# ScalarE's queue in the first feed-forward product: the activations of a unit's lower half put behind the copy of its upper half

## The chip, the cores and the metric

The kernel runs on one core of one Trainium2 chip. The metric is the device time of a whole execution in microseconds (us), lower is better. Times of engines, waits and transfers come from one profiled execution of the kernel; TensorE is called PE in the profile (its weight loads PEld), VectorE DVE, ScalarE ACT, GpSimd POOL, and SyncE, which issues the DMAs, SP (its issuing side SPq).

## The reference

128 graphs of 128 nodes with 256 features go through two layers, all in fp32. Layer 0: two rounds of graph attention (a masked softmax over a 128x128 score matrix, times the features), a residual and a layer norm, a feed-forward block with ReLU, a residual and a layer norm. Layer 1: multi-head attention with eight heads and values by relation, a residual and a norm, a feed-forward block with GELU, a residual and a norm. What the change touches is the first product of each feed-forward block and its activation:

```python
ff = jnp.matmul(jax.nn.relu(jnp.matmul(h, w_ff1) + b_ff1), w_ff2) + b_ff2        # layer 0
ff = jax.nn.gelu(x @ W1 + b1, approximate=False) @ W2 + b2                        # layer 1
```

`h` and `x` are 128 x 128 x 256, the hidden width is 1024.

## The kernel before

Four graphs make a group (`G = 4`), so there are 32 groups, and each goes through five stages: the loads, the graph attention `gat` (L421), the feed-forward block of layer 0 (`ff0`), the attention of layer 1 (L453) and the feed-forward block of layer 1 (`ff1`). Each stage is a Python generator that yields its planned duration at many points; a heap (L654 to L676) always resumes the stage whose planned time is lowest, so the stages of neighbouring groups are interleaved with a fixed period: while one group is in `ff0`, an earlier one is in attention and `ff1`, a later one in `gat`. From planned time 280 on (`kept`, L57) the PE's instructions, and SP's throughout, are tied to this order of emission by manual dependencies (L671). The queues of ACT, DVE and POOL are not tied: the framework's scheduler sets them when the program is built. The adjacency holds only 0 and 1, so the arm that runs is the one planned by `BINARY`.

The first product of a feed-forward block is a 2x2 block product with seven instead of eight block multiplications (`moving_sums`, L299, and `weight_sums` prepare the sums). Its hidden width is done in two units (`unit(0)` and `unit(2)`, L357, called u0 and u1 here), each resumed four times in turn (L358). In one unit:

- products 1 and 5 go into two PSUM tiles, `chain` and `side`; ACT copies them out (L333, L334);
- products 6, 2 and 3 follow: 6 is added onto `chain` in PSUM, 3 onto `side`. ACT copies `chain` out (L340), DVE adds the rest to make both parts of the lower half `lo` (L341, L342);
- product 7 is added onto `chain`; ACT copies it out (L345) for the second part of the upper half `hi`, which POOL completes (L346); ACT applies the activation to `lo` (L348, two instructions of 128x512);
- product 4 is added onto `chain`: it may start only when the copy of L345 has read `chain`. ACT then applies the activation to the four parts of `hi` (L354), two from `chain`, two from POOL's result.

The second product (L372) reads `lo` and `hi` of u0 first, then of u1. The same function serves both layers: in `ff0` the activation is ReLU, in `ff1` GELU. [...]before GELU and again before the exponentials of the attention (L498) a table is loaded (`ACT_TABLE_LOAD`).

Other work that the text names:

- L485, the score matmuls of the attention, PE; per group one set of 32 for its first two graphs and two of 16 for the others. Then L489 (row maxima, DVE), L498 (exponentials, ACT, 16 or 8 instructions), L502 and L503 (DVE, POOL), and the transposition of the weights by L282 (DVE), L285 (four DMAs out to DRAM) and L287 (one DMA back, tile `eT`). L517 (DVE) masks `eT`, L534 (DVE) moves the values `v` out of PSUM, and L546 (PE) multiplies `v` by the two; L550 (ACT) copies its result for L577 (PE).
- The layer norm `normalised` (L244): L250 and L251 (DVE), four short POOL instructions of which L257 is the last, and L259 (ACT, four of 128x256).
- `gat`: L429 and L437 (PE) give `wh`, which ACT copies out (L430, L438); L397 (DVE) turns one column of `wh` into `zs`, L399 (SP) writes it to DRAM and L401 reads it back over all rows; L404 (ACT) needs it, then L411 to L413 (DVE), L416 (ACT), L417 (DVE), L418 (POOL). L382 (DVE) adds the second product of a feed-forward block to the residual.

Of the kernel before, what the change touches and what calls it, by code (L numbers as in the profile page):

```python
# [214 lines left out]
def stages_of(tc, a, out, c, pools, plan):  # L215

    nc = tc.nc
# [26 lines left out]
    def normalised(y, first=0, n=G):  # L244

        y = y[:, first:first + n]
        mv = sm.tile([P, n, 2], F32, name="mv")
        for b in range(n):
            st = sm.tile([P, 6], F32, name="st")
            nc.vector.bn_stats(st, y[:, b])  # L250
            nc.vector.bn_aggr(mv[:, b], st)  # L251
        rstd = sm.tile([P, n], F32, name="rstd")
        nc.gpsimd.tensor_scalar(rstd, mv[:, :, 1], EPS, None, op0=OP.add)
        nmr = sm.tile([P, n], F32, name="nmr")
        nc.gpsimd.tensor_scalar(nmr, mv[:, :, 0], -1.0, None, op0=OP.mult)
        nc.gpsimd.tensor_tensor(rstd, rstd, c.mhalf[:, :n], OP.pow)
        nc.gpsimd.tensor_mul(nmr, nmr, rstd)  # L257
        for b in range(n):
            nc.scalar.activation(y[:, b], y[:, b], AF.Identity, bias=nmr[:, b:b + 1], scale=rstd[:, b:b + 1])  # L259

    def affine(y, k, b, n, engine=nc.gpsimd):


        for op, v in zip((OP.mult, OP.add), c.ln[k]):
            engine.tensor_tensor(y[:, b:b + n], y[:, b:b + n], v[:, None, :].to_broadcast([P, n, D]), op)  # L265
# [26 lines left out]
    def features(y, direct):  # L292

        t = t_tile().rearrange("p (b c n) -> p b c n", b=G, c=DC)
        blocks = t.rearrange("p b c n -> p (b c) n")
        transposed(y.rearrange("p b (c f) -> p (b c) f", f=P), blocks, direct, blocks)
        return t

    def moving_sums(hT):  # L299

        b11, b21, b12, b22 = (hT[:, h:h + G // 2, c] for h in (0, G // 2) for c in range(DC))
        t1, t2, t4 = (wk.tile([P, G // 2, N], F32, name=f"t{i}") for i in (1, 2, 4))
        nc.gpsimd.tensor_sub(t1, b12, b11)  # L303
        nc.gpsimd.tensor_sub(t2, b22, t1)
        nc.gpsimd.tensor_sub(b12, b22, b12)
        nc.gpsimd.tensor_sub(t4, t2, b21)
        return None, b11, b21, b22, t4, t1, t2, b12

    def feed_forward(y, before, direct, win, bin_, wout, func, by=G):


        hT = features(y, direct)
        yield TIMES["lead ff0" if before == "01" else "lead ff1"]
        hs = moving_sums(hT)
        yield TIMES["sums"]
        fT = [None] * FC

        def unit(f0):

            lo, hi = (wk.tile([P, 2, 2, T // 2], F32, name="fT", bufs=FC // 2) for _ in range(2))  # L320
            for i in range(2):
                fT[f0 + i] = lo[:, i].rearrange("p h t -> p (h t)")
                fT[FC // 2 + f0 + i] = hi[:, i].rearrange("p h t -> p (h t)")

            def product(p, k, first=False):
                for i in range(2):
                    nc.tensor.matmul(p[:, i], win[k][:, ts(f0 + i, P)], hs[k], start=first and i == 0, stop=True,  # L327
                                     skip_group_check=True)

            chain, side = (ps.tile([P, 2, T // 2], F32, name="mm") for _ in range(2))  # L330
            product(chain, 1, True)
            product(side, 5, True)
            nc.scalar.copy(lo[:, :, 0], chain)  # L333
            nc.scalar.copy(hi[:, :, 0], side)  # L334
            yield
            p = ps.tile([P, 2, T // 2], F32, name="mm")
            product(chain, 6)
            product(p, 2, True)
            product(side, 3)
            nc.scalar.copy(lo[:, :, 1], chain)  # L340
            nc.vector.tensor_add(lo[:, :, 0], lo[:, :, 0], p)  # L341
            nc.vector.tensor_add(lo[:, :, 1], lo[:, :, 1], side)  # L342
            yield
            product(chain, 7)
            nc.scalar.copy(hi[:, :, 1], chain)  # L345
            nc.gpsimd.tensor_add(hi[:, :, 1], hi[:, :, 1], hi[:, :, 0])  # L346
            for i in range(2):
                nc.scalar.activation(lo[:, i], lo[:, i], func, bias=bin_[:, f0 + i:f0 + i + 1])  # L348
            yield
            product(chain, 4)  # L350
            for h, p in enumerate((chain, hi[:, :, 1])):
                for i in range(2):
                    f = FC // 2 + f0 + i
                    nc.scalar.activation(hi[:, i, h], p[:, i], func, bias=bin_[:, f:f + 1])  # L354
            yield

        units = [unit(0), unit(2)]  # L357
        for n, now in enumerate(((0,), (1,), (0,), (1,), (0,), (1,), (0,), (1,))):  # L358
            for u in now:
                next(units[u])  # L360
            if n in (2, 4):
                affine(y, before, n - 2, 2)
            yield TIMES["ff visits"][n]
        yield TIMES["ff2"]

        late = sorted(range(FC), key=lambda f: f % (FC // 2) // 2)
        ys = [ps.tile([P, 2, D], F32, name="mm") for _ in range(G // 2)]

        def second(b, part):

            for n, f in part:
                nc.tensor.matmul(ys[b // 2][:, b % 2], fT[f][:, ts(b, N)], wout[:, f],  # L372
                                 start=b % 2 == 0 and n == 0, stop=n == FC - 1, skip_group_check=True)

        order = list(enumerate(late))
        for b in range(G):
            second(b, order[:FC // 2])
        yield TIMES["ff first half"]
        for k in range(0, G, 2):
            for b in (k, k + 1):  # L380
                second(b, order[FC // 2:])
            nc.vector.tensor_add(y[:, k:k + 2], y[:, k:k + 2], ys[k // 2])  # L382
            yield TIMES["ff half"]
            if (k + 2) % by == 0:
                normalised(y, k + 2 - by, by)
        return y
# [202 lines left out]
    def ff0(y, direct):  # L589
        return feed_forward(y, "01", direct, c.wf1_sums, c.col["bf1"], c.wf2, AF.Relu)  # L590

    def ff1(y, direct, by):
        return feed_forward(y, "11", direct, c.w1_sums, c.col["b1"], c.w2, AF.Gelu, by)
# [5 lines left out]
def layers(ctx: ExitStack, tc: tile.TileContext, a: dict, out: bass.AP, c, plan: dict):  # L599
# [3 lines left out]
    TIMES, PERIOD = plan["times"], plan["period"]  # L603
    pools = Pools(ctx, tc, plan["bufs"])
    gat_block, ff0, attention, ff1, affine, load_group = stages_of(tc, a, out, c, pools, plan)
    x0, x1, x2, loads = dict(enumerate(c.y)), {}, {}, {}

# [72 lines left out]
def graph_layers(ctx: ExitStack, tc: tile.TileContext, a: dict, out: bass.AP):  # L680
# [17 lines left out]
    with ExitStack() as start:  # L698
        tmp = start.enter_context(tc.tile_pool(name="tmp", bufs=1))
        pools = Pools(start, tc, BINARY["bufs"])  # L700
        others = constants(tc, a, c, cst, tmp, pools.ps)
        gat_block = stages_of(tc, a, out, c, pools, BINARY)[0]
        gats = [gat_block(True, f"wh{g}", g, c.xt[g], c.at[g], c.y[g]) for g in range(LEAD)]
        while gats:
            gats = [s for s in gats if next(s, None) is not None]

        words = a["adjT"].rearrange("g p b n -> (g p b n)").rearrange("(k p w) -> k p w", p=P, k=4)
        top = tmp.tile([P, 4], F32, name="top")
        for k in range(4):
            t = tmp.tile([P, words.shape[2]], I32, name="scan", bufs=3)  # L710
            nc.sync.dma_start(t, words[k])
            nc.vector.tensor_reduce(top[:, k:k + 1], t.bitcast(U32), AX.X, OP.max)
        others()
        folded(nc, c, pools.ps, c.wf1, c.col["bf1"], "01")
        c.wf1_sums = weight_sums(nc, c, c.wf1, "wf1")

        ones = tmp.tile([P, 1], F32, name="ones")
        nc.vector.memset(ones, 1.0)
        other = tmp.tile([P, 1], F32, name="other")
        nc.vector.tensor_reduce(other, top, AX.X, OP.max)  # L720
        nc.vector.tensor_scalar(other, other, 1.0, None, op0=OP.is_gt)
        p = pools.ps.tile([1, 1], F32, name="mm")
        nc.tensor.matmul(p, other, ones, start=True, stop=True)
        nc.vector.tensor_copy(flag, p)
        found = nc.values_load(flag[0:1, 0:1], min_val=0, max_val=P,
                               skip_runtime_bounds_check_because="it counts partitions")
# [54 lines left out]
```

## Time and profile before

| what | value |
|---|---|
| median of 3 runs | 2922.73 us (2919.74 to 2925.28) |
| the profiled execution | 2924.12 us, of which the span of the trace is 2922.3 us |
| mean granted PE clock | 0.978 |
| PE, DVE, ACT, POOL busy | 94%, 52%, 57%, 55% of the span |
| DMA | 328.83 MB, 49.1% of 16 engines' span |

The 40 slices of the span show PE at 90% or more from the fifth slice to the 38th; before and after these lie a start of some 90 us (loads and the first two groups alone) and an end in which nothing is left to interleave with. Between them the same pattern repeats once per group, every 84.0 to 88.1 us. A line of the timeline gives start, duration, engine, line, operation, tile written and tiles read, and in brackets how long the engine had been idle and what released it. PE's busy time is high throughout, so its few waits are what to look at.

### The profile page before, as it was taken

Reading aid. Unit: us, or ns where it says so; the run is one execution under the profiler, and the core shown is the slowest. Engines: PE = TensorE matmul, PEld = TensorE weight load, DVE = VectorE, ACT = ScalarE, POOL = GpSimd, SP = SyncE. Lnnn points to the kernel's source line nnn. Section 1 sums busy time; section 2 is a strip of 40 time slices with the busy share of each in tenths; the row PEclk is TensorE's granted clock in tenths of the full one; section 3 lists DMA queues with packets and bytes.
Section 4 is the critical chain, followed back from the end, with each engine's and each line's share of the span. In section 5 each row is a group of like instructions: output and inputs, shape, how many; then the busy total and the mean of one; then the engine's idle time right before and its main releaser. Section 6 shows DMA issues by size and latency. Waiting matters only on the chain.

```text
span 2922.3 us, 47504 instructions
## 1 busy us (share of the span) xinstructions
PE 2756.2 (94%) x16578; PEld 2146.2 (73%) x16578; DVE 1519.8 (52%) x3193; ACT 1674.7 (57%) x5127; POOL 1598.6 (55%) x1866
## 2 busy tenths in 40 slices
PE   4996999999999999999999999999999999999988
PEld 3764777777877777777777777777777777777766
DVE  5444455555544545555555565455565555455442
ACT  3445556566666565655655665656665565665543
POOL 1424555566655556655645665655566565556553
PEclk7998999999999999999999999999999999999999
DMA  7145445565455556545445555445655544554310
GB/s 274 44 105 117 100 98 112 119 135 127 109 116 109 111 117 137 113 113 119 105 106 133 121 111 119 107 108 122 134 116 115 121 107 109 125 130 107 78 37 15
DMA packets 1156955, 328.83 MB, mean 113 GB/s; under 512 B 903008, under 2 KB 1126752, under 8 KB 1156064
## 3 DMA queue, kind: packets, MB, share of 16 engines
q1 hardware_dynamic: 1156704, 325.68, 49.1%
q8 instruction: 134, 2.20, 0.3%
q14 instruction: 117, 0.96, 0.1%
HBM read 195.97 MB, written 129.62 MB: 111 GB/s over the span
## 4 chain that ended last, share of the span: by engine, by line
PE 55%; ACT 13%; DVE 11%; DMA 10%; issue 4%; SPq 4%; POOL 2%; DVEq 0%; ACTq 0%; POOLq 0%
PE mm L372 22%; PE mm L327 11%; PE mm L533 5%; ACT e L498 4%; DMA eT<-zd 4%; SPq L285 3%; PE av L546 3%; PE mm L462 3%; PE mm L469 3%; ACT tok L259 3%; PE mm L577 2%; DVE st L250 2%; DMA zd<-e 2%; DMA zd<-T 2%; PE mm L429 2%
## 5 line engine op out<-in xcount | busy, mean ns | idle before, releaser
L265 POOL TENSOR_TENSOR tok<-tok,ln_rows 128x512 f32<-128x512 f32 (+1 forms) x596 | 669.4, 1132 | 33.5 <-DVE T L282 11.5
L498 ACT ACTIVATE e<-mm,nm 128x128 f32<-128x128 f32 x1024 | 360.5, 392 | 241.4 <-DVE nm L489 225.8
L372 PE MATMUL mm<-wf,fT 128*128 128x256 f32 x2048 | 464.1, 383 | 8.6 <-ACT fT L354 7.4
L372 PE MATMUL mm<-w,fT 128*128 128x256 f32 x2048 | 460.6, 381 | 0.0
L372 PEld LDWEIGHTS mm<-wf,fT 128*128 128x128 f32 x2048 | 386.8, 191 | 73.1 <-ACT fT L354 16.1
L372 PEld LDWEIGHTS mm<-w,fT 128*128 128x128 f32 x2048 | 386.6, 190 | 70.3 <-issue 20.5
L517 DVE TENSOR_TENSOR m<-eT,am 128x1024 f32<-128x1024 f32 x128 | 184.0, 1439 | 447.6 <-DMA eT<-zd 447.4
L503 POOL TENSOR_TENSOR e<-e,s 128x512 f32<-128x512 f32 x256 | 268.5, 1057 | 253.9 <-DVE s L502 253.9
L489 DVE TENSOR_REDUCE nm<-mm 128x2 f32<-128x256 f32 (+1 forms) x384 | 171.6, 502 | 250.9 <-PE mm L485 250.9
L348 ACT ACTIVATE fT<-fT,col 128x512 f32<-128x512 f32 x256 | 170.4, 715 | 206.8 <-DVE fT L342 203.0
L259 ACT ACTIVATE tok<-tok,nmr,rstd 128x256 f32<-128x256 f32 x480 | 248.9, 590 | 46.7 <-POOL nmr L257 46.5
L418 POOL TENSOR_TENSOR e<-e,s 128x512 f32<-128x512 f32 (+1 forms) x68 | 68.1, 1003 | 342.6 <-DVE s L417 319.5
L533 PE MATMUL mm<-wv,T 128*128 128x512 f32 x512 | 247.6, 606 | 0.0
L346 POOL TENSOR_TENSOR fT<-fT 128x512 f32<-128x512 f32 x128 | 162.5, 1271 | 151.4 <-ACT fT L345 151.4
L498 ACT ACTIVATION_READ_ACCUMULATOR e<-mm,nm 128x1 f32 x1024 | 237.0, 231 | 0.0
L303 POOL TENSOR_TENSOR t<-T 128x256 f32<-128x256 f32 x64 | 47.6, 743 | 327.9 <-DMA T<-zd 327.9
L327 PE MATMUL mm<-T,w 128*128 128x256 f32 x768 | 203.9, 388 | 5.8 <-ACT fT L340 2.5
L327 PE MATMUL mm<-T,wf 128*128 128x256 f32 x768 | 193.5, 382 | 2.2 <-ACT e L498 2.1
L416 ACT ACTIVATE e<-e,nm 128x128 f32<-128x128 f32 x256 | 99.6, 390 | 160.3 <-DVE nm L413 153.9
L250 DVE BATCH_NORM_STATS2 st<-tok 128x6 f32<-128x256 f32 x480 | 177.2, 409 | 2.4
L327 PEld LDWEIGHTS mm<-T,w 128*128 128x128 f32 x768 | 144.8, 192 | 33.6 <-ACT fT L340 7.1
L327 PEld LDWEIGHTS mm<-T,wf 128*128 128x128 f32 x768 | 146.5, 191 | 23.5 <-ACT e L498 2.5
(141 smaller groups left out, 5034.9 us busy)
## 6 DMA issues: line engine op xcount, KB each, us to landing
zd<-e SPq DMA_DIRECT2D x496, 128.0 KB, 4.6
eT<-zd SPq DMA_DIRECT2D x124, 512.0 KB, 4.4
zd<-T SPq DMA_DIRECT2D x364, 128.0 KB, 3.6
T<-zd SPq DMA_DIRECT2D x91, 512.0 KB, 4.2
xt<-in_xT_dram SPq DMA_DIRECT2D x32, 512.0 KB, 5.1
e<-zsd SPq DMA_DIRECT2D x60, 256.0 KB, 3.3
tok<-in_x_dram SPq DMA_DIRECT2D x30, 512.0 KB
out_dram<-tok SPq DMA_DIRECT2D x29, 512.0 KB, 5.5
```

Source lines behind the costliest of these rows:

```text
L250: nc.vector.bn_stats(st, y[:, b])
L259: nc.scalar.activation(y[:, b], y[:, b], AF.Identity, bias=nmr[:, b:b + 1], scale=rstd[:, b:b + 1])
L265: engine.tensor_tensor(y[:, b:b + n], y[:, b:b + n], v[:, None, :].to_broadcast([P, n, D]), op)
L327: nc.tensor.matmul(p[:, i], win[k][:, ts(f0 + i, P)], hs[k], start=first and i == 0, stop=True, skip_group_check=True)
L346: nc.gpsimd.tensor_add(hi[:, :, 1], hi[:, :, 1], hi[:, :, 0])
L348: nc.scalar.activation(lo[:, i], lo[:, i], func, bias=bin_[:, f0 + i:f0 + i + 1])
L372: nc.tensor.matmul(ys[b // 2][:, b % 2], fT[f][:, ts(b, N)], wout[:, f], start=b % 2 == 0 and n == 0, stop=n == FC - 1, skip_group_check=True)
L489: nc.vector.tensor_reduce(nm[:, q].rearrange("p j i -> p (j i)"), scores[q].rearrange("p j i n -> p (j i) n"), AX.X, OP.max, negate=True)
L498: nc.scalar.activation(e[:, k], scores[q][:, j, i], AF.Exp, bias=nm[:, q, j, i:i + 1], accum_out=s[:, k:k + 1])
L503: nc.gpsimd.tensor_mul(e[:, some], e[:, some], per_row(s[:, some], N))
L517: nc.vector.tensor_tensor(m, eT, at[:, b][:, None, :].to_broadcast([P, H, N]), OP.mult)
L533: nc.tensor.matmul(p, hT[:, b, f], wv[:, f, r:r + 2], start=f == 0, stop=f == DC - 1)
```

## The change

```diff
@@ before feed_forward @@
+    def queued(later, earlier):
+        tc.add_manual_dep(later.ins, earlier.ins.name, mybir.DependencyInfo(
+            mybir.DependencyClass.NoSync, mybir.DependencyReason.DATA), reason="order of a queue")
+
@@ unit, third visit @@
             product(chain, 7)
-            nc.scalar.copy(hi[:, :, 1], chain)
+            read = nc.scalar.copy(hi[:, :, 1], chain)
             nc.gpsimd.tensor_add(hi[:, :, 1], hi[:, :, 1], hi[:, :, 0])
             for i in range(2):
-                nc.scalar.activation(lo[:, i], lo[:, i], func, bias=bin_[:, f0 + i:f0 + i + 1])
+                queued(nc.scalar.activation(lo[:, i], lo[:, i], func, bias=bin_[:, f0 + i:f0 + i + 1]), read)
```

The two activations of `lo` get a dependency on the copy of L345 that orders them on their queue and adds no semaphore. Nothing else is edited; the numbers of the lines after L308 grow by four in the changed file, and the text keeps those of the kernel before. No instruction is added or removed. SP's queue is the same. PE's queue differs in the first groups and in the last group only. The scheduler builds the queues of ACT, DVE and POOL anew. In the arm that runs, over the 27 groups in the middle, ACT's queue reads as follows (u0, u1 name the unit, A the norm of one stage and B that of the next, T the table load):

```
ff0 before, 25 blocks of 28  L340u0 L340u1 L348u0 L345u0 L259A L348u1 L345u1 L438x2 L354u0(POOL) L438x2 L259B L354u0(chain)
ff0 after, 20 of 28          L340u0 L340u1 L345u0 L348u0 L259A L345u1 L348u1 L438x2 L354u0(POOL) L259B L438x2 L354u0(chain)
ff0 after, 8 of 28           L340u0 L340u1 L345u0 L348u0 L259A L345u1 L348u1 L354u0(POOL) L438x4 L354u0(chain) L259B
ff1 before, 27 blocks        L340u0 T L348u0 L340u1 L259 L345u0 L430x2 L348u1 L550 L354u0(POOL) L345u1 L430
ff1 after, 27 blocks         L340u0 L340u1 L259 L345u0 T L348u0 L430x2 L550 L354u0(POOL) L345u1 L348u1 L430
```

DVE's queue changes in two places. After the 32 score matmuls (L485) it holds one of these orders up to the transposition L282, counted over the middle groups:

```
order a   L411 L412 L382 L413 L417 L382 L282     before 9, after 10
order b   L502 L382 L502 L411 L412 L413 L417 L382 L282     before 10, after 1
order c   L382 L411 L412 L413 L417 L382 L282     before 6, after 9
order d   L382 L502 L502 L411 L412 L413 L382 L282 ... L417     before 3, after 8
```

In the orders a, b and c, after the L534 that follows, DVE's queue before is `L397 L489 L282 L489x3 L502x2 L411 L282`; in the changed kernel it is `L282 L397 L489x4 L502x2 L282 L411` in a and c. In order d it is `L397 L489x4 L282` in both kernels. POOL's queue in `ff0` has L257 of norm B one place earlier in most blocks.

## The prediction, made before the changed kernel ran

> **What bounds the kernel now.** I read the page's busy times first, then PE's waits, then the timeline of one middle group. PE is the bound:
>
> ```profile
> PE 2756.2 (94%) x16578; PEld 2146.2 (73%) x16578; DVE 1519.8 (52%) x3193; ACT 1674.7 (57%) x5127; POOL 1598.6 (55%) x1866
> ```
>
> PE's largest wait by releaser is the one that the change aims at (total us, times, longest):
>
> ```profile
> PE mm L327 <- ACT fT L345: 41.6, 29, 1.7
> ```
>
> All 29 lie in `ff0` and hold back product 4 of u1. But the same list for the weight loads, between 1180 and 2558 us (16 groups), names a second releaser in nearly every group:
>
> ```profile
> PEld mm L327 <- ACT fT L345: 30.2, 16, 2.1
> PEld av L546 <- DVE v L534: 10.1, 15, 1.7
> ```
>
> The timeline of an `ff0` block shows why:
>
> ```profile
> 1188.72 0.38 SPq L287 DMA_DIRECT2D eT<-zd  x1
> ...
> 1193.41 1.47 DVE L517 TENSOR_TENSOR m<-eT,am 128x1024 f32<-128x1024 f32 x1 [3.12 <-DMA eT<-zd]
> ...
> 1193.78 0.56 ACT L345 COPY fT<-mm 128x512 f32<-128x512 f32 x1
> ...
> 1194.39 1.13 PE L327 MATMUL mm<-t,wf 128*128 128x256 f32 x4 [1.73 <-ACT fT L345]
> ...
> 1194.80 0.68 DVE L534 TENSOR_TENSOR v<-mm,bv 128x512 f32<-128x512 f32 x1
> 1195.54 0.42 PE L546 MATMUL av<-eT,v 128*32 128x128 f32 x8
> 1195.58 0.64 ACT L438 COPY wh<-mm 128x258 f32<-128x258 f32 x2
> ...
> 1196.22 2.08 ACT L259 ACTIVATE tok<-tok,nmr,rstd 128x256 f32<-128x256 f32 x4
> 1196.25 0.31 DVE L397 STREAM_TRANSPOSE zs<-wh 128x128 f32<-128x128 f32 x1 [0.77 <-ACT wh L438]
> ...
> 1197.44 0.86 SPq L399 DMA_DIRECT2D zsd<-zs  x1
> ```
>
> PE's next work after the delayed product, L546, needs `v`. L534 ends at 1195.48, L546 starts at 1195.54. Laid side by side, the 29 blocks give 0.05 to 0.07 us between the two in 28 of them, whether PE had waited 0.54 or 1.74 us before. So from the 32 matmuls of L485 (at 1167.8 in this group) to L546 the group is paced by the chain L498, L411 to L417, L282, the DMAs of `zd` and `eT`, L517, L534; L345 fills time that this chain would take anyway.
>
> In `ff1` PE doesn't wait, because ACT did early work in its idle time:
>
> ```profile
> 1225.64 1.28 ACT L348 ACT_TABLE_LOAD   x1
> ...
> 1230.86 1.33 ACT L348 ACTIVATE fT<-fT,col 128x512 f32<-128x512 f32 x2 [3.94 <-DVE fT L342]
> ...
> 1232.10 0.56 ACT L340 COPY fT<-mm 128x512 f32<-128x512 f32 x1
> ...
> 1232.35 0.20 POOL L257 TENSOR_TENSOR nmr<-nmr,rstd 128x4 f32<-128x4 f32 x1
> ...
> 1232.59 2.07 ACT L259 ACTIVATE tok<-tok,nmr,rstd 128x256 f32<-128x256 f32 x4
> ...
> 1234.57 0.56 ACT L345 COPY fT<-mm 128x512 f32<-128x512 f32 x1
> ...
> 1237.87 0.58 ACT L345 COPY fT<-mm 128x512 f32<-128x512 f32 x1
> ...
> 1239.04 1.03 PE L327 MATMUL mm<-t,w 128*128 128x256 f32 x4
> ```
>
> The table load and u0's activations are done before L257 frees the norm L259. The second L345 ends at 1238.45, product 4 of u1 starts at 1239.04: 0.6 us of slack.
>
> [...]ACT stood 3.94 us before L348 with L340 of u1 behind it, whose product ended before 1229. [...]The trace shows 1.28 us, but where the next activation was ready (load 2855.17, L348 2856.46) it followed at once[...]. [...]Here an L265 that takes 1.27 us alone took 2.27 beside L517. I use this for norm B below.
>
> **Part 1, the wait in `ff0`.** L345 of u0 moves into ACT's idle 3.35 us before 1188.87 and L345 of u1 in front of two L348: product 4 of u1 can start near 1192.9 instead of 1194.39. L546 stays at 1195.54, as L517 still waits for `eT`. Gain at L546: 0. After it, PE's wait of 0.38 us on L354 mostly goes: ACT's busy run from 1190.1 to 1198.2 is one L345 (0.47 us from start to start) shorter. That is 0.35 us a group, if nothing later sets the end.
>
> **Part 2, the order on DVE.** The period of a group, from one set of 32 L485 to the next, depends on the order in which DVE does L382: 85.85 us in order a, 85.93 in b, 85.37 in c, 84.0 to 84.7 (mean 84.27) in d, in groups where nothing else was late. The counts go from a 9, b 10, c 6, d 3 to a 10, b 1, c 9, d 8: 85.85 - 9 x 85.93 + 3 x 85.37 + 5 x 84.27 = -10 us.
>
> **Part 3, the table load in `ff1`.** L348 of u0 now stands behind its L345, that behind L259, and L259 can't start before L257 (1232.35). So ACT idles from about 1227.9 to 1232.6, and the load and L348 of u0 come afterwards. By starts in the trace the run from L259 to the end of L345 of u1 was 1.98 + 0.46 + 0.54 (L430) + 1.24 (L348) + 0.25 (L550) + 0.81 (L354) + 0.58 = 5.86 us. The new one has L348 of u0 for that of u1, plus 1.28 for the load and 0.1 for its not overlapping L345: 7.24. L345 of u1 ends at 1239.83, product 4 starts at 1239.9: 0.86 late. L577, one place ahead, waits for L550 (1238.8) on the way. The slacks of the other orders give 0.57 in c, 0.95 in d. Behind the waiting product stand L462, L469 and L372 on PE, which had no other wait, so this counts in full.
>
> **Part 4, `zs` in orders a to c.** ACT now does norm B ahead of the second pair of L438, and DVE has L282 of norm B's result ahead of L397. L257 of norm B ends by about 1195.0 (held by L517), L259 runs from 1195.3 to 1197.4, L282 to 1198.65, and L397 comes at 1198.65 instead of 1196.25. L399, which stood behind another load until 1197.44, goes out at 1199.0: 1.5 us late. On SP everything behind it shifts: L401 waits for L399's landing (1201.91), then four L285, L287, two loads, four L285, and L287 of the next `eT`; DVE waited 3.47 us for that at 1223.24 (L517). Behind L517 stand L250, L449 and L251 of the very norm whose L257 frees L259 in `ff1`. Groups in which L517 was 1.2 to 1.5 us later than here had L257 1.9 later. Bounds for a: 0.86 (nothing carries) to 0.86 + 1.9 = 2.8; for c 0.57 to 1.4. Not every microsecond need pass through five links; I take 2.3 for a and b, 1.1 for c, 0.95 for d.
>
> **Sum.** 11 x 2.3 + 9 x 1.1 + 8 x 0.95 = +43. Some middle groups of before already ran 86.4 to 87.7 us with a late L257, and paid about 6 us of this: -6. Part 2: -10. Part 1 is swallowed, since L259's chain and not PE sets product 4 in `ff1`. First groups and last group, with other PE orders: 0, within 3 either way. Net +27 on the profiled execution's 2924.1 (span 2922.3 and 1.8 around it): 2951; the median of before lies 1.4 below, so 2950.
>
> **Rivals.** *The wait is pure gain:* 41.6 us less, 2882. For it: the page's largest wait of PE. Against: L534 ends just ahead of L546 in 28 of 29 blocks. Chance 0.07. *The other side, the norm is early enough:* if L257 in `ff1` ended before 1231.7 (0.65 us sooner; 0.5 to 0.9 by order), the load would fall into idle time again. Then parts 1 and 2 stay: -10 and 20 x 0.35 = -7, about 2906. The order d helps it, but there PE arrives sooner too. 0.15. *No carry:* L397 is late, but SP's slack takes it. 11 x 0.86 + 9 x 0.57 + 8 x 0.95 - 10 = +12, about 2935. 0.2. *The parts cancel* within 0.2% (5.8 us, about what a measurement of this kernel can tell from no change), 2917 to 2928: 0.13. That the change does not do what it says is excluded by the built queues.
>
> **Numbers.** My case, 2938 to 2966 by its own bounds, has 0.45; with no carry 0.65 for slower. Same 0.13, faster 0.22. The range leaves out the pure gain below and, above, a full carry[...]: 2906 to 2967.
>
> **What would show it.** PE's wait on L345 in `ff0` nearly gone, with L546 waiting about as long for L534 instead; a new wait of PE on L345 or L550 in `ff1`, 1 to 2.5 us a group; ACT's table load after L259 and back to back with L348; L397 some 2.4 us later after L546 in orders a and c; periods of 87 to 89 us in these and about 85 in d. I am wrong if L546 moves up with product 4, or if PE has no wait in `ff1`.

## The result, and the profile after

The changed kernel took 2957.88 us (median of 4 runs, 2948.32 to 2963.28) against 2922.69 us (median of 4 runs). The ratio is 1.0117, 95% interval 1.0089 to 1.0145: slower by 1.2%, which is more than noise. The forecast was 2950. The profiled execution has a span of 2957.1 us, 34.8 more than before, and a mean granted PE clock of 0.972 instead of 0.978.

No instruction was added on PE, and yet its busy time grew by 34.3 us, nearly as much as the span:

```profile
PE 2790.5 (94%) x16578; PEld 2167.6 (73%) x16578; DVE 1519.4 (51%) x3193; ACT 1677.0 (57%) x5127; POOL 1602.0 (54%) x1866
```

A count of idle time alone can't explain that, so I cut every group at five PE instructions and added up the pieces. The 27 groups used are those whose `ff0` block has the ordinary shape; outside them the kernel gets 1.7 us shorter. "Half clock" is the time lost while the trace records a granted clock of 0.5 (half the recorded length).

| stretch of a group, sum of 27 groups, us | before | after | change |
|---|---|---|---|
| first of the 32 L485 to first L546 | 744.3 | 735.4 | -8.9 |
| L546 to the last of the first 32 L372 of `ff0` | 245.9 | 270.2 | +24.3, of it half clock +18.4 |
| from there to the first L327 of `ff1` | 428.6 | 428.6 | 0 |
| `ff1`: first L327 to product 4 of u1 | 507.9 | 526.2 | +18.3 |
| product 4 of u1 to the next L485 | 397.7 | 400.5 | +2.8 |
| sum | 2324.4 | 2360.9 | +36.5 |

Next, the waits of PE by releaser in the changed kernel (total us, times, longest). Lines behind L308 carry numbers that are four higher: L349 is L345, L489 is L485, L550 is L546, L538 is L534, L442 is L438, L581 is L577.

```profile
PE av L550 <- DVE v L538: 43.6, 30, 4.9
...
PE mm L489 <- ACT wh L442: 10.5, 17, 0.6
PE mm L581 <- ACT oT L554: 10.0, 16, 1.9
```

The line that the change aimed at is gone, and its 41.6 us stand under another name: PE now waits for `v`, 43.6 us. Sorted by the order on DVE, L546 starts 27.6 us after L485 in order a, 27.15 in c and 26.55 in d, in both kernels (medians). Removing the wait moved nothing there.

The `ff0` block of one group of order a in the timeline (start, duration, engine, line, operation, tiles, and in brackets the idle time before it):

```profile
1033.05 1.67 DVE L521 TENSOR_TENSOR m<-eT,am 128x1024 f32<-128x1024 f32 x1 [2.91 <-DMA eT<-zd]
1033.60 1.18 POOL L257 TENSOR_TENSOR nmr<-nmr,rstd 128x4 f32<-128x4 f32 x1
...
1034.64 0.68 DVE L538 TENSOR_TENSOR v<-mm,bv 128x512 f32<-128x512 f32 x1
...
1035.13 2.07 ACT L259 ACTIVATE tok<-tok,nmr,rstd 128x256 f32<-128x256 f32 x4
...
1035.37 0.43 PE L550 MATMUL av<-eT,v 128*32 128x128 f32 x8 [1.52 <-DVE v L538]
...
1036.38 0.50 PE L489 MATMUL mm<-kT,T 32*128 32x128 f32 x6
...
1037.10 0.63 ACT L442 COPY wh<-mm 128x258 f32<-128x258 f32 x2
...
1037.51 1.22 PE L489 MATMUL mm<-kT,T 32*128 32x128 f32 x10 [0.64 <-ACT wh L442]
...
1038.66 9.68 PE L376 MATMUL mm<-wf,fT 128*128 128x256 f32 x32
```

Two things are new here. The seventh of the score matmuls L489 needs a PSUM buffer that the second pair of L442 has to empty; that pair now stands behind the norm L259, which runs until 1037.2, and so PE stops for 0.64 us in the middle of L489. And the 32 matmuls L376 take 9.68 us. In the same group of the kernel before, the 32 ran from 1025.42 to 1033.23, 7.81 us with a wait of 0.37 in them:

```profile
1025.42 1.13 PE L372 MATMUL mm<-wf,fT 128*128 128x256 f32 x4
...
1026.92 6.31 PE L372 MATMUL mm<-wf,fT 128*128 128x256 f32 x28 [0.37 <-ACT fT L354]
```

The starts of the single matmuls show why: from the second to the twelfth of the changed kernel they are 0.43 us apart, from the thirteenth on 0.22, as nearly all of them were before. The busy times by stretch confirm it (the column after POOL's is the granted PE clock):

```profile
core 0: us, PE busy (x) PEld busy (x) DVE busy (x) ACT busy (x) POOL busy (x), PEclk, DMA share, GB/s
1034.00:1037.40 3.40, 1.51 (x38) 1.12 (x38) 1.48 (x3) 3.40 (x10) 3.40 (x4) 0.93 0.49 70
1037.40:1044.20 6.80, 6.69 (x24) 5.42 (x25) 2.93 (x8) 5.64 (x25) 5.43 (x5) 0.53 0.56 164
```

The same stretch of the same group in the kernel before:

```profile
1025.90:1032.70 6.80, 6.43 (x31) 5.32 (x30) 2.61 (x7) 5.91 (x25) 5.05 (x5) 1.00 0.70 202
```

PE counts as busy in both; after the change it does 24 matmuls in that time instead of 31, at a clock of 0.53. That is how busy time grows without work. It isn't the whole of the growth: of the 32.0 us of added busy time in the 27 groups, 21.7 lie in this stretch, and 12.7 in `ff1` and behind it, at full clock (below). Of the 27 groups, three in the kernel before and eight in the changed one lose 1.7 or 3.4 us this way.

The `ff1` block of the same group:

```profile
1075.43 0.20 POOL L257 TENSOR_TENSOR nmr<-nmr,rstd 128x4 f32<-128x4 f32 x1
...
1075.67 2.07 ACT L259 ACTIVATE tok<-tok,nmr,rstd 128x256 f32<-128x256 f32 x4 [4.14 <-POOL nmr L257]
...
1077.65 0.56 ACT L349 COPY fT<-mm 128x512 f32<-128x512 f32 x1
...
1078.23 1.28 ACT L352 ACT_TABLE_LOAD   x1
...
1079.53 1.34 ACT L352 ACTIVATE fT<-fT,col 128x512 f32<-128x512 f32 x2
...
1081.29 0.38 ACT L554 COPY oT<-av 128x256 f32<-128x256 f32 x1
...
1081.72 0.73 PEld L581 LDWEIGHTS mm<-wo,oT 128*128 128x128 f32 x4 [0.48 <-ACT oT L554]
...
1082.36 0.59 ACT L349 COPY fT<-mm 128x512 f32<-128x512 f32 x1
...
1083.00 0.73 PEld L331 LDWEIGHTS mm<-t,w 128*128 128x128 f32 x4 [0.55 <-ACT fT L349]
```

ACT idles for 4.14 us, then does the norm, the first L349, the table load and L352 in a row, and PE waits twice behind it, 0.48 us for L554 and 0.55 for the second L349. As the loads of weights wait and not the matmuls, the list of matmul waits shows little of it: L577 starts 1.10 us after the matmuls ahead of it and product 4 of u1 1.28 us after L577, instead of 0.86 us each in the same group before, and only 0.07 and 0.15 us of that count as idle. So here, too, the profile counts PE as busy while it waits.

### The profile page after: what moved, and what is told of

It is laid out like the page before. It is cut to its first block, busy times and chain, and to the rows that moved or that the text cites. A ratio compares the mean times of both kernels' runs of the same rounds, so it can differ in the third digit from the quotient of the medians.

```text
span 2957.1 us, 47496 instructions
## 1 busy us (share of the span) xinstructions
PE 2790.5 (94%) x16578; PEld 2167.6 (73%) x16578; DVE 1519.4 (51%) x3193; ACT 1677.0 (57%) x5127; POOL 1602.0 (54%) x1866
## 4 chain that ended last, share of the span: by engine, by line
PE 49%; ACT 19%; POOL 12%; DVE 8%; DMA 6%; issue 4%; SPq 1%; ACTq 0%; DVEq 0%; POOLq 0%
PE mm L376 24%; PE mm L331 7%; POOL tok L265 6%; ACT e L502 5%; ACT tok L259 4%; PE mm L473 4%; PE mm L466 4%; DMA eT<-zd 3%; PE mm L537 3%; PE mm L489 3%; ACT fT L352 2%; POOL rstd L256 2%; PE av L550 2%; DMA zd<-e 1%; PE mm L581 1%
## 5 line engine op out<-in xcount | busy, mean ns | idle before, releaser
L265 POOL TENSOR_TENSOR tok<-tok,ln_rows 128x512 f32<-128x512 f32 (+1 forms) x596 | 654.1, 1108 | 26.4 <-DVE T L282 11.4
L376 PE MATMUL mm<-wf,fT 128*128 128x256 f32 x2048 | 475.9, 392 | 0.0
L376 PE MATMUL mm<-w,fT 128*128 128x256 f32 x2048 | 460.6, 381 | 0.0
L376 PEld LDWEIGHTS mm<-wf,fT 128*128 128x128 f32 x2048 | 400.6, 197 | 62.3 <-ACT fT L358 1.8
L376 PEld LDWEIGHTS mm<-w,fT 128*128 128x128 f32 x2048 | 386.6, 190 | 70.1 <-issue 20.3
L259 ACT ACTIVATE tok<-tok,nmr,rstd 128x256 f32<-128x256 f32 x480 | 249.2, 592 | 183.4 <-POOL nmr L257 182.0
L303 POOL TENSOR_TENSOR t<-T 128x256 f32<-128x256 f32 x64 | 47.6, 744 | 270.2 <-DMA T<-zd 270.2
L282 DVE STREAM_TRANSPOSE T<-tok 128x1024 f32<-128x1024 f32 x87 | 108.0, 1241 | 140.0 <-ACT tok L259 140.0
L352 ACT ACTIVATE fT<-fT,col 128x512 f32<-128x512 f32 x256 | 171.3, 720 | 11.9 <-DVE fT L346 9.3
L282 DVE STREAM_TRANSPOSE e<-e 128x1024 f32<-128x1024 f32 x124 | 152.4, 1230 | 28.8 <-POOL e L507 28.8
```

Of the source, the lines that this page charges most:

```text
L282: nc.vector.transpose(z, y)
L352: queued(nc.scalar.activation(lo[:, i], lo[:, i], func, bias=bin_[:, f0 + i:f0 + i + 1]), read)
```

## The experiments

Each kernel was timed beside the kernel before on the same chip; the chips differ (the kernel before had medians of 2913.7 to 2914.9 us on those used here), so ratios are compared. In all of them the helper stands on lines that were empty, so their line numbers are those of the kernel before. All compute the whole of the reference. An order on a queue is made as in the change, by a dependency without a semaphore.

### The two layers apart

```diff
-        queued = lambda later, earlier: tc.add_manual_dep(
+        queued = lambda later, earlier: func == AF.Relu and tc.add_manual_dep(
```

> The new order in the ReLU layer alone; the GELU layer keeps its old queue. Theory (two separate costs): in ff0 PE now waits inside L485 for the second pair of L438 (about +0.47 us in the groups of orders a and c), TensorE drops to half clock beside that wait in some groups (about +19 us in all), the better mix of DVE orders gives back 9, and ff1 loses nothing because its table load is early again: 2922.7 + 6 + 19 - 9 = 2939, range 2930 to 2945, with lost clock of some 20 us more than before in the middle groups. Rival (the loss sits in ff1, the clock is chance): about 2914, below the kernel before.

Measured: 1.0036, interval 1.0024 to 1.0049. The waits of PE show L485's stop as expected:

```profile
PE mm L485 <- ACT wh L438: 13.1, 19, 2.2
```

In `ff1` product 4 of u1 came after 18.5 us in 17 of the 18 groups of orders a and c, as before the change: with L397 as late as in the changed kernel (30.1 to 30.6 us), nothing of that lateness reached product 4. The lost clock was 8.5 us, not 20. So `ff0` alone costs something, its sign as expected, its size smaller.

With `AF.Gelu` in the place of `AF.Relu`:

> The new order in the GELU layer alone. Theory: from the start of the ff1 block to product 4 of u1 18.5 us become 19.1 to 19.4 in every middle group, 0.1 us more behind it, no lost clock: 27 x 0.7 = +19, so 2942, range 2936 to 2946. Rival (the late norm in ff1 was made in ff0 and the table load alone is hidden): within 5 us of 2922.7.

Measured: 1.0082, interval 1.0058 to 1.0106. From the start of `ff1` to product 4 the 27 groups took 528.4 us instead of 507.9, and 2.8 us more behind it, a little more than expected; lost clock 3.4 us, all of it outside `ff1`. L397 stayed where it was in the kernel before (medians of 28.3 and 28.4 us in orders a and b). The rival falls: the table load costs by itself, without any late norm.

### The norm behind the pair of copies

L259 of norm B, the attention's norm, gets a dependency on the fourth L438 of the group beside it (`norm_b` holds the four L259 with their group's number):

```diff
-        normalised(y)
+        normalised(y); norm_b[:] = [(g, i) for i in last_norm.values()] if binary else []
...
-            nc.scalar.copy(wh[:, b, :D + 2], p)
+            pair = nc.scalar.copy(wh[:, b, :D + 2], p)
-        yield TIMES["gat copy"]
+        [tc.add_manual_dep(i.ins, pair.ins.name, ...) for k, i in norm_b if k == g - 3]; yield TIMES["gat copy"]
```

> The changed kernel, with the norm L259 of ff0's stage B held behind all four L438, as it stood before. Theory: L485 no longer waits for L438, L397 comes 2.2 us earlier again, and with no wait between L485's matmuls TensorE keeps its full clock: the 25 us of the ff0 block go, the 20 us of ff1 stay: 2933, range 2928 to 2940, lost clock in the middle groups under 7 us. Rival (the clock drops because product 4 moved away from the idle time ahead of L546, whatever L485 does): lost clock stays near 24 us and the time at 2950 or more.

Measured: 1.0036, interval 1.0025 to 1.0048, so some 0.8% less than the changed kernel. The middle groups lose no clock at all, of L485's waits on L438 one of 0.2 us is left, and L546 to the end of the first 32 L372 took 237.1 us, 8.8 less than in the kernel before, which had half clock in three of these groups. Product 4 of u1 starts 24.7 to 25.0 us after L485 here, as in the changed kernel, with the idle 1.5 us behind it; that alone does not lower the clock here. In `ff1` the way to product 4 takes 535.0 us, 8.8 more than in the changed kernel, though `zs` is early again: PE arrives there sooner, and the norm hardly does.

### The table load brought back

```diff
+            pre = lambda: nc.scalar.activation(sm.tile([P, 1], F32, name="pre"), bin_[:, :1], func) if func == AF.Gelu and f0 == 0 else None
...
-            product(chain, 7)
+            pre(); product(chain, 7)
```

> The changed kernel, with one more GELU of a 128x1 column, whose result nobody reads, issued on ACT ahead of L340 in ff1: it brings the table load back into ACT's idle time, and every other queue stays as it is. Theory: L345 of u1 comes 1.28 us earlier, PE's way to product 4 returns to 18.5 us except in groups with a late L257: 27 x 0.6 = 16 us less, 2942, range 2936 to 2948. Rival (the late norm and not the table sets product 4): less than 5 us gained, above 2952.

Measured: 1.0039, interval 1.0023 to 1.0055, more than expected. The timeline of ACT in the `ff1` block of one group of order a:

```profile
1058.62 1.28 ACT L319 ACT_TABLE_LOAD   x1
1059.92 0.20 ACT L319 ACTIVATE pre<-col 128x1 f32<-128x1 f32 x1
1060.03 0.57 ACT L340 COPY fT<-mm 128x512 f32<-128x512 f32 x1
1061.47 0.59 ACT L340 COPY fT<-mm 128x512 f32<-128x512 f32 x1 [0.88 <-PE mm L327]
1067.11 1.09 ACT L259 ACTIVATE tok<-tok,nmr,rstd 128x256 f32<-128x256 f32 x2 [5.05 <-POOL nmr L257]
```

The load lies ahead of the 5.05 us in which ACT waits for the norm, and costs nothing. Product 4 came after 18.5 us in the median of all three orders, 503.8 us in all. The twelve executions took 2917.51 to 2939.96 us, and the profiled one, with 2939.96, lost 29.0 us of clock in the middle groups, 23.9 of it in order c, where the changed kernel lost most in orders a and b (22.2 of 23.9). The lost clock is therefore not bound to one order, and what this kernel gained by the median is more than this profile shows.

### Useless work between the narrow matmuls

```diff
             scores = [ps.tile([P, n, DC, N], F32, name="mm") for _ in range(HC)]
+            if binary and bs[0] == 2:
+                nc.tensor.matmul(scores[0][:, 0], c.wo[:, 0, :P], hT[:, 0, :], start=True, stop=True, skip_group_check=True)
```

> The changed kernel, with one more matmul of 128x256 on PE between L546 and L485 of the first pair (its result is overwritten at once and read by nobody; 0.43 us of useless work a group). Theory (the clock drops when the wait ahead of L546, the narrow matmuls L546 and L485 and the wait inside L485 join into one stretch[...]): the stretch is cut in two, the groups of order a keep their full clock or lose much less, and the kernel with more work is faster than the changed one: lost clock in the middle groups under 10 us instead of 24, ratio to before 1.003 to 1.008 instead of 1.0117. Rival (clock has to do with total idle time or with chance): lost clock 20 us or more, ratio 1.011 to 1.016.

Measured: 1.0097, interval 1.0078 to 1.0117. The time expected was missed. The clock was not: 1.7 us lost in the middle groups instead of 23.9, mean clock 0.980. The timeline of one group of order a (the added matmul is L480):

```profile
1029.29 0.43 PE L546 MATMUL av<-eT,v 128*32 128x128 f32 x8 [1.53 <-DVE v L534]
...
1030.30 0.70 PE L480 MATMUL mm<-T,wo 128*128 128x256 f32 x2
1030.93 1.21 PE L485 MATMUL mm<-kT,T 32*128 32x128 f32 x16
...
1032.06 6.31 PE L372 MATMUL mm<-wf,fT 128*128 128x256 f32 x28
```

PE waits 1.53 us before L546 as in the changed kernel, and L485 ends no sooner, but L372 runs at full speed: 28 in 6.31 us. By the trace, the clock stays up when 0.43 us of work a group that nobody reads is added. By the times, the interval overlaps that of the changed kernel, so a gain in time is likely and not shown. The edit also moved ACT's and DVE's queues in some blocks (15 groups of order a and 12 of d instead of 10 of a and b, 9 of c and 8 of d), so the matmul is not all that differs, and in d it costs its time (9.09 us instead of 8.62 from L546 to the last of the first L372).

### The kernel once more, and with both repairs

> The changed kernel once more, beside a kernel with both repairs. Theory: the half clock belongs to this order of work and not to one execution: lost clock in the middle groups 15 to 28 us again, mostly in groups of order a, ratio to before 1.009 to 1.014. Rival (it was chance): lost clock under 8 us, ratio 1.004 to 1.008.

Measured for the changed kernel: 1.0133, interval 1.0110 to 1.0156; lost clock 27.3 us in the middle groups, mean clock 0.970. The size was as expected, the place was not: order c lost 20.5 us of it and a 6.8.

The other kernel has the norm behind the pair and the early table load, with the change in both layers:

> The changed kernel, in both layers, with the norm of stage B behind all four L438 and the unread GELU of 128x1 that loads the table early. Theory (the loss is the table load in ff1 plus, in ff0, L485's wait and the clock that falls beside it, and nothing else): both go, and what stays is the gain of the change in ff0: ratio 0.993 to 0.998, as in the kernel with the change in ff0 alone and the norm held back; product 4 of u1 in ff1 after 18.5 us in most groups. Rival (the late norm in ff1 costs on its own): ratio 1.001 to 1.004.

Measured: 0.9944, interval 0.9928 to 0.9960. Lost clock 1.7 us; L546 to the end of the first L372 238.0 us (before 245.9), product 4 of `ff1` 505.6 us (before 507.9). With the two repairs the whole loss is gone, and a gain of half a per cent appears; 11.4 of the 21.2 us less in the 27 groups lie ahead of L546, in the mix of DVE orders.

### What the change gains when nothing is in its way

This kernel has the change in the ReLU layer alone and the norm behind the pair.

> The change in ff0 alone, with the norm of stage B behind all four L438. Theory: only the gains remain: 12 us at L546 through the better mix of DVE orders, 0.4 us a group behind it (8.7 instead of 9.1 us to the end of L372's first half), no lost clock, and in ff1 the old queue, where some groups pay up to 1 us because PE arrives sooner while the norm doesn't: ratio 0.990 to 0.996 to the kernel before. Rival (what ff0 gains is taken back whole by the late norm in ff1): 0.997 to 1.002.

Measured: 0.9956, interval 0.9939 to 0.9972. L546 sits where it was by orders (27.60, 27.13, 26.51), L546 to the end of the first L372 takes 8.71 us in order a instead of 9.10, without loss of clock. Of the 19.9 us less in the 27 groups, 11.2 lie ahead of L546, where the mix of orders sets the time, and 9.4 behind it, where the kernel before had half clock in three groups and this one has none. So the change in `ff0` is worth these 0.4 us in orders a to c; the mix is a by-product of the new build, and "The order on DVE" below gets more of it without the change (21.2 us ahead of L546).

The next two put `v` in front of the mask on DVE: L517 gets a dependency on L534. The first is the kernel before with that alone.

```diff
-                nc.vector.tensor_tensor(m, eT, at[:, b][:, None, :].to_broadcast([P, H, N]), OP.mult)
+                behind(nc.vector.tensor_tensor(m, eT, at[:, b][:, None, :].to_broadcast([P, H, N]), OP.mult))
```

> The kernel before, with L517 queued behind L534 on DVE, so that v no longer stands behind the wait for eT. Theory (L546 waited for v, with product 4 close behind it): L546 moves from 27.7 to about 27.5 us, where product 4 and so L345 now sets it; PE's wait on L345 stays at 1.7 us: ratio 0.997 to 1.000 from this, moved by the mix of orders. Rival (v was not what L546 waited for): L546 stays at 27.7 in order a.

Measured: 0.9951, interval 0.9934 to 0.9967, faster than expected, though PE still waited for L345 29 times (34.5 us). With `v` early, L546 follows product 4 without a wait, and starts 0.1 us sooner in every order (27.5 to 27.6, 27.05 and 26.4 us): L345 takes over as its bound at nearly the same time. The gain is the mix, 12, 8 and 7 groups in orders a and b, c and d instead of 18, 6 and 3, and the half clock, of which the middle groups lost none. In `ff1` 9.5 us are given back (517.4 us to product 4 instead of 507.9).

The second adds it to the kernel with the norm behind the pair.

> As the change in ff0 alone with the norm of stage B behind L438, and L517 behind L534 on DVE besides. Theory: with product 4 early and v early, L546 waits for the mask L517 only and starts at about 27.05 instead of 27.6 us in order a, 0.6 us a group less: 27 x 0.6 = 16 us less than without it where ff1's norm allows it, ratio 0.985 to 0.992. Here, and not in the change itself, the removed wait on L345 pays. Rival (ff1's norm sets the period): within 4 us of the kernel without the order on DVE.

Measured: 0.9948, interval 0.9931 to 0.9964, the same as without this order. L546 did start earlier, at 25.9 us, and gave it back at once. The waits of PE:

```profile
PE mm L372 <- ACT fT L354: 16.6, 21, 0.8
PE mm L437 <- POOL e L418: 16.4, 4, 8.9
PE av L546 <- DVE m L517: 15.8, 25, 1.8
```

The second half of L546 waits for the mask, and L372 for L354 on ACT. From L485 to the last of the first L372 the 27 groups took 971.0 us against 969.6 without the order. My expectation of 16 us was wrong. Its rival named the time (3.5 us between the medians) and not the reason: `ff1`'s way to product 4 is as long as without the order (508.8 and 508.6 us). The waits on L354, which the kernel without it does not have among its largest, point to ACT's run of activations as what stands behind `v`.

### The order on DVE

Part 2 of the forecast took the period's dependence on the order from a correlation. Here the order is made, in 22 groups: L417 (`inverse`) gets a dependency on the L282 (`turn`) of the first attention weights.

```diff
-        eT = [turned(es[0])]
+        eT = [turned(es[0])]; binary and 5 < g < 28 and [tc.add_manual_dep(i.ins, turn[0].ins.name, ...) for i in inverse]; inverse.clear()
```

> The kernel before, with L417, the reciprocal that waits for the exponentials L416, queued behind the transposition L282 on DVE in the middle groups. Theory (the order of DVE sets the start of L546): L282 starts at 12.5 to 13.3 instead of 14.26 us in order a, L546 at 26.4 to 27.1 instead of 27.7: some 0.8 us in 19 groups and 0.4 in 5: 17 us less, ratio 0.991 to 0.997. Rival (the orders only go along with the period): L546 stays where it was, ratio 0.999 to 1.001.

Measured: 0.9933, interval 0.9912 to 0.9954. The timeline of DVE in one of these groups:

```profile
1001.46 0.69 DVE L413 TENSOR_REDUCE nm<-e 128x4 f32<-128x512 f32 x1
1002.07 0.68 DVE L382 TENSOR_TENSOR tok<-tok,mm 128x512 f32<-128x512 f32 x1
...
1002.66 1.24 DVE L282 STREAM_TRANSPOSE e<-e 128x1024 f32<-128x1024 f32 x1
1003.93 0.18 DVE L417 RECIPROCAL s<-s 128x4 f32<-128x4 f32 x1
```

L282 follows L382, and L417 with its wait for L416's exponentials comes behind. L546 starts at 25.9 to 26.8 us in 20 of the 22 groups (median 26.66), and the way to it took 723.1 us instead of 744.3. The order is a cause.

> The change in ff0 alone, the norm of stage B behind L438, and L417 behind L282. Theory: L546 at 26.3 to 26.9 us in all middle groups, product 4 ready before it; 0.4 us a group behind it as without L417's move: ratio 0.986 to 0.993, the fastest of all. Rival (ff1's norm comes no sooner and takes it back): 0.994 to 0.998.

Measured: 0.9906, interval 0.9887 to 0.9925, median 2885.96 us against 2914.16: the fastest of all, faster than both kernels. It holds the change in the first layer, the norm behind the pair, and L417 behind L282. L546 starts at 25.6 to 26.9 us in the 22 groups (median 26.5).

## Why the forecast was right, and where it was not

The sign was right and 2957.88 lies in the range. The sum of +27 us on the profiled execution met +34.8. Its terms did not all hold: 21 us that did not come were made up for by 18.4 us of half clock and 5.9 us behind L546 that it did not have. That the number came out so near is luck in this part; the mechanism held at the main points of parts 1 to 3.

| term of the forecast | forecast, us | measured, us | shown by |
|---|---|---|---|
| part 1, L546 held by the chain of `v` | 0 | 0 | L546 by orders, both kernels |
| part 1, after L546 | 0 (0.35 a group, swallowed) | +5.9 | L485's wait on L438 |
| part 2, mix of orders on DVE | -10 | -8.9 (up to L546) | first row of the table; L417 moved by itself |
| part 3, table load in `ff1`, less late groups | 22.2 - 6 = 16 | 18.3 + 2.8 = 21.1 | `ff1` alone; the early load |
| part 4, `zs` carried into `ff1` | +21 | about 0 | `ff1` alone; times from L399 to L257 |
| half clock | not in it | +18.4 | clock records; norm behind pair; useless work |
| first and last groups | 0 | -1.7 | table |

- *Part 1 held at its main point.* The page's largest wait of PE was worth nothing, since L534 ends just ahead of L546. What it lacks belongs to the sentence on the time after it: "PE's wait of 0.38 us on L354 mostly goes". It went, but I had used the later second pair of L438 only for `zs` on DVE (part 4), and not asked who else waits for those copies: the PSUM buffers of L485 do. The 0.35 us came out where the pair was put back.
- *Part 3 held.* 0.86 and 0.57 us were named for orders a and c; the medians of the way to product 4 rose by 0.65 and 0.60, and by 0.1 behind it. Order d lost 1.43 instead of 0.95. In the `ff1` block shown above the load takes 1.28 us and L352 starts 0.02 us after its end: the forecast's 1.28 us for the load held.
- *Part 4 is the step that failed.* L397 did come 2.2 us late (30.6 us against 28.4), and L399 at 30.9, near the 31.2 named. But "I take 2.3 for a and b, 1.1 for c" presumed that lateness passes five links. With the table load early, product 4 of `ff1` doesn't move though `zs` is as late as ever; that alone could be slack. But with the change in `ff1` alone, `zs` on time, the way to product 4 is no shorter (528.4 us against 526.2), and the trace shows where the lateness went. In the groups of order a without half clock (three after the change, nine before; medians, counted from L485), L399 comes 1.7 us later than before (30.9 against 29.3), L401 0.8 (34.5 against 33.6), the next L287 0.5 (50.7 against 50.2), L517 0.3 (55.3 against 55.1) and L257 0.5 (64.9 against 64.4). Half of it is gone at L401, and what reaches L257 is no more than PE itself is late at the start of `ff1` (53.05 against 52.6). The 21 us were an error, hidden by the half clock that I had not seen coming.
- *The rivals.* Pure gain and an early enough norm are out. "No carry" (about 2935) described the norm rightly; the clock and L485 make up the rest.

## What to carry to other kernels

A long wait that ends just ahead of another operand's arrival is worth nothing: compare the end of every other input with the start of the next instruction before counting it. When an order on a queue is edited, list all readers of each instruction that slides back, the reuse of its PSUM buffer among them, and look at where idle time held a table load. And where a change lengthens a stretch in which PE does little, compare starts of equal matmuls and the granted clock: the busy share did not show the half speed here (6.69 of 6.80 us busy at a clock of 0.53).

## What the runs showed of the hardware

*The recorded drops of the PE clock lie on a grid.* All recorded drops to 0.5 (18 in the kernel before, 22 in the changed one) begin at whole multiples of 3.413 us from one another, within 0.2% of such a window, and those in the middle groups last one or two of them (3.413 or 6.827 us). I counted the matmuls that start in each full-clock window of the changed kernel, of its repetition, of the kernel with the early table and of that with `ff0` alone. Of windows with no full-size matmul (128*128 in the profile) and fewer than the 48 narrow ones of one attention step (L546 is 128*32 there, L485 32*128), 27 of 27 were followed by half clock; with none and all 48, 1 of 8; with one or two full-size ones and at least 35 narrow ones, none of 23.

In other kernels a drop did follow two windows with one full-size and 32 or 40 narrow ones (the added matmul; `v` first with the pair), and in all kernels together eleven windows with one to five full-size and at most 19 narrow ones, in which PE was idle for 1.7 to 2.6 us. These are counts of what was seen; whether a fixed limit lies behind them, and where, was not measured.

In the group shown above the drop is recorded from 1036.93 us on, for two windows. In the window before it PE waited 1.52 us ahead of L550 and started 38 narrow matmuls and no full-size one; its wait of 0.64 us in L489 begins 0.06 us ahead of the drop.

The grid does not begin with the kernel: its first line lies 2.70 us after the start in the changed kernel's execution and 3.20 us in its repetition's. That another group meets it badly in each execution fits the spread of the changed kernel (2943 to 2963 us at clocks of 0.977 to 0.970 in its repetition), but was not tested by itself. The changed kernel was hit at equal distances (511.3, 774.1, 1036.9 and 1299.8 us, 77 windows or 262.8 us apart); three of its groups take 262.7 to 263.9 us there, so the same stretch came back to nearly the same place of the grid.

*A tiny POOL instruction beside a large DVE one.* L257 of 128x4 took 1.18 us in the `ff0` block shown above, beside the mask L517 of 1.67 us, and 0.20 us in the same group of the kernel before, where it ran behind L517. In both kernels together, the 27 L257 that began while an L517 was running took 1.18 to 1.20 us and ended 0.06 us behind it; the five that began 0.04 to 0.18 us ahead of one took 0.20 us.
